# Query projections: block product 6 by seven smaller products, the first query weights scaled on GpSimd

## The chip, the cores and the metric

The kernel runs on one core of one Trainium2 chip. The metric is the device time of one execution in microseconds. The profiler's records of one execution are the profile; its times count from the span's start. The engines are TensorE (PE for its matmuls, PEld for its weight loads), VectorE (DVE), ScalarE (ACT), GpSimd (POOL) and SyncE (SP), which issues most of the DMAs.

## The reference

A cross-attention block and a feed-forward block on 8 batches of 128 tokens, width 512, all in float32 (cut to what matters here):

```python
x = x + xattn(layernorm(x), ctx, mask, ...)     # 32 heads of 128
x = x + ffn(layernorm(x), Wg, Wu, Wd, ag, au, ad)

def xattn(hidden, kv, mask, position_bias, ln_weight, w_q, w_k, w_v, w_out):
    x = rmsnorm(hidden) * ln_weight
    h_q = (x @ w_q.T).reshape(b, lq, 32, 128)   # 512 -> 4096
    h_k = (kv @ w_k.T).reshape(b, lk, 32, 128)
    h_v = (kv @ w_v.T).reshape(b, lk, 32, 128)
    score = softmax(where(mask, h_q . h_k + position_bias, -inf))
    return hidden + (score . h_v).reshape(b, lq, 4096) @ w_out.T
```

The change lies in `h_q`: the projection of the 1024 normalized tokens by `w_q`, whose rows are scaled by `ln_weight`.

## The kernel before

**Block products.** A product of a weight matrix (512 features by 512 columns of one group of four heads) with the tokens (512 features by 1024 tokens) is cut into 2 by 2 blocks and formed from seven block products rather than eight, numbered 1 to 7, with sums of the weights' blocks (`sums_a`, L299: s1, s2, s4 and a21 in place) and of the tokens' blocks (`sums_b` and `token_sums`: t1, t2, t4 and b12 in place). Each block product contracts 256 features, so it is two tiles of 128 head columns, each two matmuls of 128x128 weights by 512 tokens. Products add up in PSUM: product 6 is added to product 1 and so on, and copies or adds take the partial sums out to the head tiles.

A block product may be cut once more in the same way: `inner` (L383) forms it from seven smaller products of 128 by 256 tokens, in seven steps, in the order 2, 1, 5, 6, 3, 7, 4. The steps write two banks in turn (`two` for 2, 5 and 3, `one` for 1, 6, 7 and 4), and after each step VectorE adds the bank to the head. Steps 6, 7 and 4 accumulate on what step 1 left in `one`; steps 5 and 3 in `two` likewise, step 5 starting it anew. So no step can write its bank before VectorE has read the previous step of that bank.

**The stages around the change.** In `first_kv` TensorE forms keys and values of group 0 from the context. Beside it the first norm runs: for each pair of batches VectorE takes moments and small factors of 128x2, ScalarE scales the tokens (`hn`), VectorE transposes each batch in blocks of 32x32, and SP writes the result to DRAM (`turned`) and reads it back turned (`hT`), one batch after another in one queue. When batches i and i+4 are there, VectorE forms the token sums (`h_sums`). All this is in an order written out by hand: `InOrder` keeps each engine's instructions in program order, and tables such as `moments_at` and `sums_at` say behind which tile of `first_kv` each piece comes. ScalarE scales the query weights of group 0 (`weigh_q`, tiles 17 to 20); GpSimd forms their block sums (`combine_rows`) at tile 21.

**The query stage** runs over the eight groups. For group 0 `whole` forms products 1, 6 and 7 in full; for later groups it forms 1 and 6 in full, and `inner_T7` forms product 7 by seven smaller ones. Products 2 to 5 are always formed by smaller ones: `inner_T` forms all four at once, step by step (`quads`, seven steps of four matmuls and three adds each), and its steps run during the next group: one behind each of the four tiles of `whole`, one behind the second, fourth and sixth step of product 7. GpSimd forms the weight sums for the next group meanwhile: four of 128x512 in `combine_rows`, four of 128x128 for product 7 and eight of 128x256 for products 2 to 5 (`pair_rows`); before that ScalarE scales that group's weights in four parts. The sums lie in tiles of the tags of the attention stage, two sets in turn by the group's parity (`q_rows`). The token sums for product 7 (four instructions on VectorE) are formed in group 1, behind the first tile. Finished heads of the group before are stored to DRAM (`store_queries`); three of the four value tiles of group 0 are kept in DRAM meanwhile and come back at the stage's end.

Around the stage, SP's queue carries the weights of the next group, the stores of heads, the first loads of queries and the bias tiles of the attention stage, in program order as buffers come free.

```python
steps = [(i, *blocks[i]) for i in (2, 1, 5, 6, 3, 7, 4)]
for i, r, c in steps:
    for m, (ns, place) in zip(two if i in (2, 5, 3) else one, places):
        for h, n in enumerate(ns):
            multiply(n, i, m[:, h], i in (2, 1, 5) and h == 0)
```

## Time and profile before

| | us |
|---|---|
| median of 3 runs | 1066.57 (1066.43 to 1066.77) |
| the profiled execution | 1067.09 |
| its span, first to last instruction | 1065.2 |
| PE busy | 1055.4 |
| DVE busy | 742.1 |
| ACT busy | 315.5 |
| POOL busy | 521.4 |
| query stage (first query matmul to first key matmul of group 1) | 57.02 to 233.75 |

The granted TensorE clock was full over the whole span. A timeline row gives the start, the time to the last end, the engine, the line, the operation, the tiles written and read, the shape and how many instructions were merged; brackets give the engine's idle time before the row and what ended it. Line L60 is that of the helper that keeps the order, so many instructions carry it; they are told apart by their tiles (`i_q`: banks of products 2 to 5, `sc_q` and `av_q`: the two banks of product 7, `mm_q`: banks of whole products). One float32 matmul is recorded as two passes, so two rows of 128x256 are one matmul.

### The profile page before, as it was taken

What the parts mean: (1) busy time and instruction counts of PE and PEld (TensorE: products, weight loads), DVE (VectorE), ACT (ScalarE), POOL (GpSimd) and SP (SyncE); (2) the same over time, 40 slices, a digit from 0 to 9 for tenths busy, and PEclk for the clock granted to TensorE, in tenths of its full rate; (3) what the DMA queues carried; (4) which work ended last, traced back from release to release, by engine and by line L of the source; (5) the groups of instructions that cost most, each with busy time, mean ns of one, the idle gap of its engine ahead of it and who ended that gap; (6) DMA issues with size and microseconds to landing.
All of it is one profiled execution on the core that took longest, in us unless ns stands there. A gap on an engine that the chain in (4) does not pass through costs nothing.

```text
span 1065.2 us, 14597 instructions
## 1 busy us (share of the span) xinstructions
PE 1055.4 (99%) x5114; PEld 837.6 (79%) x5114; DVE 742.1 (70%) x1362; ACT 315.5 (30%) x874; POOL 521.4 (49%) x551
## 2 busy tenths in 40 slices
PE   9999999999999999999999999999999999999998
PEld 5657777775889798888889769998888865666887
DVE  4686666697778787787787766884544337889852
ACT  2632122205544434444444433221000012333100
POOL 6446664616855565555652275670000336997010
PEclk9999999999999999999999999999999999999999
DMA  9533444386555554564656557774541632110011
GB/s 291 184 134 119 158 161 156 119 289 231 172 199 188 169 179 168 187 199 161 206 171 196 175 202 235 242 254 136 181 138 60 191 108 60 41 54 5 1 40 40
DMA packets 125560, 165.00 MB, mean 155 GB/s; under 512 B 15696, under 2 KB 77392, under 8 KB 125488
## 3 DMA queue, kind: packets, MB, share of 16 engines
q1 hardware_dynamic: 111072, 132.87, 37.8%
q10 hardware_dynamic: 12544, 24.38, 6.5%
q0 software_dynamic: 1872, 6.82, 2.1%
q8 instruction: 41, 0.67, 0.3%
q14 instruction: 31, 0.25, 0.1%
HBM read 106.38 MB, written 57.67 MB: 154 GB/s over the span
## 4 chain that ended last, share of the span: by engine, by line
PE 90%; DVE 4%; DMA 4%; ACT 1%; issue 1%; ACTq 0%; SPq 0%; POOL 0%; DVEq 0%; POOLq 0%
PE i_q L60 9%; PE m L904 9%; PE m L60 7%; PE mm_v L504 7%; PE mm_k L483 7%; PE i_v L432 7%; PE d L1459 6%; PE i L1324 6%; PE i_k L402 6%; PE mm_q L60 5%; PE mm_f L1364 5%; PE av L583 4%; PE sc L537 4%; PE mm_k L60 2%; PE sc_q L60 1%; PE sc L60 1%
## 5 line engine op out<-in xcount | busy, mean ns | idle before, releaser
L60 DVE TENSOR_TENSOR q<-q,i_q 128x512 f32<-128x512 f32 x168 | 94.8, 596 | 52.6 <-PE i_q L60 50.6
L522 POOL TENSOR_TENSOR s<-pb,mneg 128x512 f32<-128x512 f32 x40 | 61.6, 1539 | 90.8 <-DVE p L561 72.1
L550 ACT ACTIVATE s<-s,nmx 128x128 f32<-128x128 f32 x240 | 93.3, 390 | 32.8 <-DVE nmx L545 23.7
L397 DVE TENSOR_TENSOR v<-v,i_v 128x512 f32<-128x512 f32 (+1 forms) x126 | 73.6, 588 | 32.2 <-PE i_v L432 20.0
L588 ACT COPY aT<-av 128x512 f32<-128x512 f32 x60 | 35.1, 585 | 164.3 <-PE av L583 129.7
L397 DVE TENSOR_TENSOR k<-k,i_k 128x512 f32<-128x512 f32 (+1 forms) x105 | 59.8, 587 | 24.7 <-PE i_k L402 24.3
L60 POOL TENSOR_TENSOR s<-pb,mneg 128x512 f32<-128x512 f32 x24 | 36.8, 1534 | 69.5 <-DVE p L561 28.0
L537 PEld LDWEIGHTS sc<-k,q 128*128 128x128 f32 x416 | 53.8, 192 | 6.7 <-issue 4.1
L376 ACT COPY q<-mm_q 128x512 f32<-128x512 f32 x36 | 20.9, 586 | 124.1 <-PE mm_q L60 124.1
L537 PE MATMUL sc<-k,q 128*128 128x128 f32 x416 | 55.3, 275 | 0.0
L504 PE MATMUL mm_v<-wv,ctx_sb 128*128 128x256 f32 x224 | 52.5, 379 | 0.0
L483 PE MATMUL mm_k<-ctx_sb,wk 128*128 128x512 f32 x112 | 52.4, 593 | 0.0
L301 DVE TENSOR_TENSOR S_a<-a 128x256 f32<-128x256 f32 x22 | 9.3, 424 | 57.7 <-DMA a<-att 32.5
L60 PE MATMUL m<-wo,a 128*128 128x256 f32 x200 | 48.5, 380 | 0.8 <-DMA a<-att 0.8
L583 PE MATMUL av<-pT,v 128*128 128x128 f32 x368 | 48.6, 275 | 0.0
L904 PE MATMUL m<-wo,a 128*128 128x256 f32 x200 | 48.4, 379 | 0.0
L1099 POOL TENSOR_TENSOR x<-x,u 128x256 f32<-128x256 f32 x4 | 3.0, 752 | 90.8 <-DVE x L1098 90.8
L60 POOL TENSOR_TENSOR S_q<-wq 128x512 f32<-128x512 f32 x8 | 10.2, 1270 | 75.0 <-ACT wq L60 75.0
L504 PEld LDWEIGHTS mm_v<-wv,ctx_sb 128*128 128x128 f32 x224 | 41.5, 190 | 5.1
L550 ACT ACTIVATION_READ_ACCUMULATOR s<-s,nmx 128x1 f32 x240 | 44.8, 187 | 0.0
L583 PEld LDWEIGHTS av<-pT,v 128*128 128x128 f32 x368 | 44.8, 192 | 0.0
L561 DVE TENSOR_TENSOR p<-s,ri 128x512 f32<-128x512 f32 x52 | 43.5, 836 | 0.9
(408 smaller groups left out, 2735.1 us busy)
## 6 DMA issues: line engine op xcount, KB each, us to landing
queries<-q SPq DMA_DIRECT2D x32, 512.0 KB, 3.5
turned<-tt SPq DMA_DIRECT2D x64, 256.0 KB, 2.4
pT<-turned SPq DMA_DIRECT2D x64, 256.0 KB, 2.9
att<-aT ACTq DMA_DIRECT2D x64, 256.0 KB, 3.0
q<-queries SPq DMA_DIRECT2D x30, 512.0 KB, 4.9
a<-att SPq DMA_DIRECT2D x23, 512.0 KB, 4.1
wq<-in_wqT_dram SPq DMA_DIRECT2D x8, 1024.0 KB, 6.9
wk<-in_wkT_dram SPq DMA_DIRECT2D x7, 1024.0 KB, 5.6
```

Source lines behind the costliest of these rows:

```text
L60: return self.tc.keep_in_program_order(getattr(self.engine, op)(*args, **kw))
L397: vector.tensor_tensor(to, *(base or [to]), out, ADD)
L402: kv_tensor.matmul(out, a[n][i], b[n][i], start=first, stop=True, skip_group_check=True)
L432: kv_tensor.matmul(out[:, bass.ts(k, S)], b[n][i][:, bass.ts(k, S)], a[n][i], start=first and k == 0, stop=True, skip_group_check=True,)
L483: kv_tensor.matmul(out, w[i][:, c, bass.ts(t, P)], src[i][:, c, :], start=(first and c == 0), stop=(c == HC - 1), skip_group_check=True,)
L504: kv_tensor.matmul(out[:, bass.ts(k, HW)], src[i][:, c, bass.ts(2 * t + k, S)], w[i][:, c, :], start=(first and k == 0 and c == 0), stop=( ...
L537: tensor.matmul(sc[:, j, :], qT[:, j, bass.ts(b % 2, S)], kT[j][:, cols], start=True, stop=True)
L550: scalar.activation(s[:, j, :], s[:, j, :], AF.Exp, bias=nmx[:, j : j + 1], accum_out=sm[:, j : j + 1],)
L583: tensor.matmul(av[:, j, :], v[b // 2][:, b % 2, bass.ts(j, P)], pT[:, :, j, :], start=True, stop=True,)
L904: tensor.matmul(m[n], sa[n][:, c, :], wo_t[g][n][:, c, :], start=(g == order[0] and c == 0 and PRODUCTS.index(n) % 2 == 0), stop=(g == ord ...
L1324: nc.tensor.matmul(out, a[n][k], fine_t[n][k], start=first, stop=True, skip_group_check=True)
L1459: nc.tensor.matmul(out, lhs, rhs, start=bank not in started, stop=(i == NP - 1 or n == 8), skip_group_check=True,)
```

## The change

Three things change.

- Product 6 is formed by seven smaller products in all groups but the first (`inner_T6`, in the banks of the whole products), so `whole` forms product 1 alone there. The steps of products 6 and 7 and of the previous group's `quads` (0) are interleaved by a list. The token sums for products 6 and 7 (eight instructions) are formed where those for 7 were.
- GpSimd scales the weights of group 0 itself, at tile 16 of `first_kv`, and forms their block sums and the finer sums right behind it.
- The sums lie in other tiles: other tags for both sets, one more token-sum tile; all four value tiles are kept in DRAM rather than three. The scaling of the next group's weights is placed at other points of the group.

```diff
+    def inner_T6(name, a, b, heads):
+        def place(r, c, m, first):
+            left, to = (heads[r - 1][:, bass.ds(at + (c - 1) * HW, HW)] for at in (0, 512))
+            return [(to, left if first else to, m[:, 0])]
+
+        banks = [[ps_mm.tile([P, 2, HW], F32, tag="mm", name=f"m6{k}_{name}")] for k in range(2)]
+        return inner(name, multiply_T(a, b), (((6,), place),), banks, True)
...
+    q_rows = [row_space((("aT", 2), ("aT", 2), ("pb", 2)), (("s4", 1), ("p", 1)))]
+
+    def q_inner_rows(g, w):
+
+        pieces, single = q_rows[g % 2]
+        a = {}
+        for n in (6, 7) if g else ():
+            quarters = [w[n][:, c, bass.ts(r, P)] for r in range(2) for c in range(2)]
+            a[n] = sums_a(gpsimd, *quarters, *(single[n][:, k] for k in range(3)))
+        a.update(pair_rows(w, pieces))
+        return a
...
-        if 17 <= n < 17 + DC:
-            weigh_q(q_w[0], n - 17)
-        if n == 21:
+        if n == 16:
+            for c in range(DC):
+                gpsimd.tensor_tensor(
+                    q_w[0][:, c], q_w[0][:, c],
+                    lnw_sb[:, c : c + 1].to_broadcast([P, GW]), ALU.mult,
+                )
             rows_q = combine_rows("q0", q_w.pop(0))
+            a_q0 = q_inner_rows(0, rows_q)
...
-            for i in range(1, B // 2):
-                nc.sync.dma_start(kept[i - 1], v[i])
+            for i in range(B // 2):
+                nc.sync.dma_start(kept[i], v[i])
+            q_rows.append(row_space(3 * (("pT", 4),), 2 * (("tt", 2),)))
...
-        tiles = whole(name, *blocks_T(name, w, h_t, heads), 2 if g else 3)
-        a = q_inner_rows(g, w)
+        tiles = whole(name, *blocks_T(name, w, h_t, heads), 1 if g else 3)
+        a = q_inner_rows(g, w) if g else a_q0
...
             if g == 1 and k == 0:
-                h_inner.update(inner_tokens(vector, h_t, 8, q_place, (7,)))
-            if g + 1 < NG and k >= 2:
-                weigh_q(q_w[g + 1], k - 2)
-        for k, _ in enumerate(inner_T7(name, a, h_inner, heads)) if g else ():
-            if k in (1, 3, 5):
-                next(quads)
...
+                h_inner.update(inner_tokens(vector, h_t, 8, q_place, (6, 7)))
+            if g == 0 and k >= 2:
+                weigh_q(q_w[1], k - 2)
+        if g:
+            streams = {
+                6: inner_T6(name, a, h_inner, heads), 7: inner_T7(name, a, h_inner, heads), 0: quads
+            }
+            for k, n in enumerate((6, 6, 0, 6, 6, 0, 7, 6, 0, 7, 6, 0, 6, 7, 7, 0, 7, 7, 7)):
+                next(streams[n])
+                if g + 1 < NG and k in (2, 5, 8, 11):
+                    weigh_q(q_w[g + 1], k // 3)
+                if g + 1 < NG and k == 11:
+                    rows_now = combine_rows(f"q{g + 1}", q_w.pop(g + 1))
+                if k == 15:
+                    store_queries(g - 1, heads_before)
```

More of the change, by code (lines that the diff above doesn't have):

```diff
@@ L701, in weigh_q, with spare, row_space @@
         InOrder(tc, nc.scalar).mul(w[:, c], w[:, c], lnw_sb[:, c : c + 1])
+    def spare(tag, bufs, shape=(2, 2, P)):
+        return work.tile([P, *shape], F32, tag=tag, name=f"rows_{tag}", bufs=bufs)
+    def row_space(tags, single):
+        tiles = [spare(*t) for t in tags]
+        sevens, sixes = (spare(*t, (3, P)) for t in single)
+        return [t[:, k] for t in tiles for k in range(2)], {7: sevens, 6: sixes}
+    q_rows = [row_space((("aT", 2), ("aT", 2), ("pb", 2)), (("s4", 1), ("p", 1)))]
[7 more added lines that the diff above has]
+        return a
     moments_at, roots_at = {7: 0, 8: 1, 10: 2, 12: 3}, {8: 0, 9: 1, 11: 2, 13: 3}
@@ L760, in xattn_ffn_kernel @@
     v = kvs[0][1]
-    kept = [dram.tile([P, 2, GW], F32, name=f"v0_kept_{i}") for i in range(1, B // 2)]
-    def spare(tag, bufs, shape=(2, 2, P)):
-        return work.tile([P, *shape], F32, tag=tag, name=f"rows_{tag}", bufs=bufs)
+    kept = [dram.tile([P, 2, GW], F32, name=f"v0_kept_{i}") for i in range(B // 2)]
     def q_place(n):
-        if n == 7:
-            pieces = [t[:, k] for t in q_seven for k in range(2)]
-        else:
-            pieces = [t[:, k] for t in q_sums for k in range(4)][3 * (n - 2) :]
-        t1, t2, t4 = pieces[:3]
-        return t1, t2, h_t[n][:, 0, slice(8, None)], t4
-    def q_inner_rows(g, w):
-        pieces, single = q_rows[g % 2]
-        a = {}
-        if g:
-            quarters = [w[7][:, c, bass.ts(r, P)] for r in range(2) for c in range(2)]
-            a[7] = sums_a(gpsimd, *quarters, *(single[:, k] for k in range(3)))
-        a.update(pair_rows(w, pieces))
-        return a
+        t1, t2, t4 = q_sums[3 * (n - 2) :][:3]
+        return t1, t2, h_t[n][:, 0, slice(8, None)], t4
     quads, rows_now, h_inner = iter(()), rows_q, {}
@@ L790, in xattn_ffn_kernel @@
         if g == 0:
-            for i in range(1, B // 2):
-                nc.sync.dma_start(kept[i - 1], v[i])
+            for i in range(B // 2):
+                nc.sync.dma_start(kept[i], v[i])
+            q_rows.append(row_space(3 * (("pT", 4),), 2 * (("tt", 2),)))
             q_sums = [
-                acts.tile([P, 4, 8, BS], F32, tag="a", name=f"t_q{k}") for k in range(3)
-            ]
-            even, odd = [spare("s", 3) for _ in range(3)], [spare("tt", 2) for _ in range(2)]
-            odd.append(spare("aT", 2))
-            q_rows = [
-                ([t[:, k] for t in tiles for k in range(2)], single)
-                for tiles, single in (
-                    (even, spare("s4", 1, (3, P))), (odd, spare("aT", 2, (4, P))),
-                )
-            ]
-            q_seven = [
-                work.tile([P, 2, 8, BS], F32, tag="pT", name=f"t_q7{k}", bufs=4) for k in range(2)
-            ]
+                acts.tile([P, 4, 8, BS], F32, tag="a", name=f"t_q{k}") for k in range(4)
+            ] + [work.tile([P, 2, 8, BS], F32, tag="pT", name="t_q", bufs=4)]
+            q_sums = [t[:, k] for t in q_sums for k in range(t.shape[1])]
         w, heads, name = rows_now, [], f"q{g}"
-        tiles = whole(name, *blocks_T(name, w, h_t, heads), 2 if g else 3)
-        a = q_inner_rows(g, w)
+        tiles = whole(name, *blocks_T(name, w, h_t, heads), 1 if g else 3)
+        a = q_inner_rows(g, w) if g else a_q0
         for k, _ in enumerate(tiles):
@@ L818, in xattn_ffn_kernel @@
             if g == 1 and k == 0:
-                h_inner.update(inner_tokens(vector, h_t, 8, q_place, (7,)))
-            if g + 1 < NG and k >= 2:
-                weigh_q(q_w[g + 1], k - 2)
-        for k, _ in enumerate(inner_T7(name, a, h_inner, heads)) if g else ():
-            if k in (1, 3, 5):
-                next(quads)
-            if g + 1 < NG and k in (0, 2):
-                weigh_q(q_w[g + 1], 2 + k // 2)
-            if k == 2 and g + 1 < NG:
-                rows_now = combine_rows(f"q{g + 1}", q_w.pop(g + 1))
-            if k == 5:
-                store_queries(g - 1, heads_before)
+                h_inner.update(inner_tokens(vector, h_t, 8, q_place, (6, 7)))
[13 more added lines that the diff above has]
+                    store_queries(g - 1, heads_before)
         if g == 0:
@@ L839, in xattn_ffn_kernel @@
     store_queries(NG - 1, heads)
-    for i in range(1, B // 2):
+    for i in range(B // 2):
         v[i] = acts.tile([P, 2, GW], F32, tag="a", name=f"v0_back_{i}")
-        nc.sync.dma_start(v[i], kept[i - 1])
+        nc.sync.dma_start(v[i], kept[i])
     gpsimd, vector, kv_tensor = nc.gpsimd, nc.vector, nc.tensor
```

## The prediction

> **What bounds the kernel now.** I read the page first, then the busy time by stretch, then the rows of TensorE, VectorE and GpSimd by time where the change works.

> ```profile
> PE 1055.4 (99%) x5114; PEld 837.6 (79%) x5114; DVE 742.1 (70%) x1362; ACT 315.5 (30%) x874; POOL 521.4 (49%) x551
> PE 90%; DVE 4%; DMA 4%; ACT 1%; issue 1%; ACTq 0%; SPq 0%; POOL 0%; DVEq 0%; POOLq 0%
> ```

> TensorE works nearly without a break. The edited query stage lies from 57.02 to 233.75 us; by stretch (sum, then busy PE, PEld, DVE, ACT, POOL):

> ```profile
> 67.33:89.30 21.97, 21.97 (x88) 16.34 (x86) 16.72 (x30) 6.66 (x12) 19.54 (x25) 1.00 0.12 49
> 111.27:133.25 21.98, 21.98 (x88) 16.34 (x87) 14.27 (x29) 4.81 (x8) 12.26 (x17) 1.00 0.40 144
> ```

> A group takes 21.97 us and PE is busy for all of it: no slack on PE, 5 to 8 on DVE. So a matmul less is time gained, and a wait of PE is time lost; nothing later takes it back.

> ```profile
> 131.95 0.59 PE L60 MATMUL i_q<-t_q,wq 128*128 128x256 f32 x2
> 132.38 0.59 PE L60 MATMUL i_q<-t_q,S_q 128*128 128x256 f32 x2
> 132.82 0.59 PE L60 MATMUL sc_q<-t_q,wq 128*128 128x256 f32 x2
> ```

> Each row is one 128x256 matmul (two passes), 0.43 us from start to start; a 128x512 one takes 0.86.

> **Part 1, fewer matmuls.** Product 6 of a group was 4 matmuls of 128x512, 3.44 us; now it is 7 of 128x256, 3.02 us. Seven groups: 7 x 0.43 = 3.0 us gained. Two ACT copies per group go (0.59 each), seven DVE adds come (0.41 each, as on product 7's banks): DVE goes from 14.3 to 17.2 us of some 22, no bound by itself. Four more GpSimd sums of 128x128 (0.46 each) make its 12.3 us about 14.1; the scaling ahead of them is no longer behind product 6's copies, so they start earlier. All hidden under 22 us of PE.

> **Part 2, the new order of steps.** The seven steps go (2, 1, 5, 6, 3, 7, 4). The last two accumulate in one bank: DVE must have read it after step 7 before PE may run step 4. Before, product 7 ran 7 7 Q 7 7 Q 7 7 Q 7 (Q: a step of the previous group's block sums, 1.72 us on PE), so a Q stood between. Now the list ends 7 7 Q 7 7 7: steps 3, 7, 4 back to back.

> ```profile
> 133.02 1.02 DVE L60 TENSOR_TENSOR q<-q,i_q 128x512 f32<-128x512 f32 x2 [0.17 <-PE i_q L60]
> 133.95 0.41 DVE L60 TENSOR_TENSOR q<-q,sc_q 128x256 f32<-128x256 f32 x1
> ```

> Let T be the time when Q's last matmul has its turn behind it (132.82 above). DVE gets Q's second half at T+0.20 and is through at T+1.13 (133.02, 133.95). The add of step 3 follows, then that of step 7, 0.33 apart as on the two product-7 banks at 131.36 and 131.69: step 7's starts at T+1.46 and ends at T+1.87. PE starts 0.05 behind a DVE read (read ended 231.60, matmul 231.65), at T+1.92; it was ready at T+0.86. It waits 1.06 us in each of seven groups, 7.4 us, and behind it on PE stands the next group's product 1. Bounds: were DVE idle, step 7's result would come at T+1.06 and the wait be 0.66 (4.6 in all); with dependent adds 0.52 apart (126.18 to 126.70, same banks) 1.43 (10.0). I take 1.06, since those two banks' adds go to different heads. Parts 1 and 2 together: +4.4 (+1.6 to +7.0).

> That PE does stop for this, in the tail where no product 7 lies between:

> ```profile
> 231.08 0.59 PE L60 MATMUL i_q<-hT,S_q 128*128 128x256 f32 x2
> 231.65 0.70 PE L60 MATMUL i_q<-t_q,wq 128*128 128x256 f32 x2
> ```

> 0.57 in place of 0.43, even with 0.86 us of the other half's matmuls as cover.

> **Part 3, GpSimd scales the first query weights.** ACT loses 4 x 0.66 us that nobody waited for. GpSimd was idle from 28.78 to 43.75; the weights landed at 24.25. Now four scalings (taken as the 128x512 row, 1.26), four sums of the same size and eight of 128x256 (0.73) fill 28.8 to about 44.6. That moves GpSimd's work off the h sums at 47.45 to 55.9, and onto norm 1's small VectorE instructions:

> ```profile
> 26.45 1.11 DVE L60 SCALAR_TENSOR_TENSOR nm<-mv,rr 128x2 f32<-128x2 f32 x1
> ...
> 29.21 0.17 DVE L60 TENSOR_SCALAR rr<-mv 128x2 f32<-128x2 f32 x1
> 29.29 0.16 DVE L60 RECIPROCAL rr<-rr 128x2 f32<-128x2 f32 x1
> 29.48 0.16 DVE L60 SCALAR_TENSOR_TENSOR nm<-mv,rr 128x2 f32<-128x2 f32 x1
> ```

> The same instruction takes 0.16 us with GpSimd idle and 1.11 with GpSimd busy: it ended at 27.56, just behind a GpSimd row that ended at 27.54. Four such lie ahead of the first transpose (29.21, 29.48, 31.29, 31.56). With GpSimd rows ending every 1.24 us they end at about 30.0, 31.2, 33.65 and 35.0, and the first transpose starts at 34.9, not 31.64: +3.3 us. Behind it SP's queue writes and reads the transposed blocks through DRAM with no slack: blocks 3, 4 and 5 landed at 45.3, 47.4 and 49.9, 2.3 apart, so block 5 lands at 49.9 + 3.3 = 53.2. DVE forms three h sums on it (0.57 each) before it may add v (0.68) and free PE's bank: 55.6.

> ```profile
> 47.45 5.30 DVE L60 TENSOR_TENSOR hT<-hT 128x256 f32<-128x256 f32 x6 [3.19 <-DMA hT<-turned]
> 53.49 3.69 PE L60 MATMUL mm_v<-S_v,ctx_sb 128*128 128x256 f32 x16 [1.32 <-DVE v L60]
> ```

> PE was ready at 52.17 and waited 1.32 us, since these six sums took 5.30 us with GpSimd beside them where the next six took 3.42. It would now wait 3.5: +2.2. Bounds: without the delay, 49.9 + 1.7 + 0.7 = 52.3, a wait of 0.15, -1.2; with a whole 1.27 for each of the four, 5.1 of delay, +4.0. Taken: +2.2.

> **Part 4, token sums for product 6.** In the first step of group 1 DVE now forms eight sums, not four, while GpSimd works:

> ```profile
> 71.97 1.44 DVE L60 TENSOR_TENSOR t_q<-hT 128x256 f32<-128x256 f32 x1
> 73.45 1.38 DVE L60 TENSOR_TENSOR t_q<-hT,t_q 128x256 f32<-128x256 f32 x1
> 74.75 0.67 DVE L60 TENSOR_TENSOR hT<-hT 128x256 f32<-128x256 f32 x1
> ```

> From the group's start (67.33 above): they begin at +4.64; two at 1.4 beside long GpSimd rows, six at 0.6 beside short ones: done at +11.0. Then Q's adds (1.54) and product 6's step 2 (0.41): +13.0. PE reaches product 6's step 5, which overwrites that bank, at 2 x 1.72 + 2 x 1.72 + 2 x 0.43 + 1.72 = +9.46. Wait 3.5 us, behind which everything on PE stands; before, PE had product 6 whole as cover and did not stop. Bounds: eight at 0.42 (no GpSimd): 0.5; all at 1.44: 8.7. I take 3.5, GpSimd's sums of 128x128 being short.

> [...]

> **Moved and added DMAs.** One more 512 KB store of v and one more load: the first pair of loads landed by 235.0, first use at 257.93; 20 us of cover. One bias load now waits for a sum tile and stands on SP ahead of group 6's stores, but its tile is free before those stores' data is. Cost 0; if the cover were gone, one load's pace, 1.3 us.

> **Sum.** 4.4 + 2.2 + 3.5 = +10.1 on the profiled execution: span 1065.2 to 1075.3. That execution took 1067.09 us, 0.5 above the median of 1066.57. Forecast for the median: 1076.7.

> **Rivals.**
> - *The count decides* (8%): PE finds the bank read, because DVE runs further ahead than I think. It decides once the wait per group is under 0.43 us. Then -3.0, and with the h sums free of GpSimd -1.2: 1062.4, faster. For it: DVE has slack over a group. Against it: the wait is one DVE latency at least, 0.66.
> - *GpSimd's early work disturbs nothing* (12%): the small instructions slip in between; -1.2 in place of +2.2 and 0.5 in place of 3.5: 4.4 - 1.2 + 0.5 = +3.7, 1070.3. For it: 0.17 us instructions need little. Against: three rows of 0.93 to 1.11.
> - *DVE falls behind in every group* (10%): from product 6's step 2 on, PE has 5 x 1.72 + 14 x 0.43 = 14.6 us of work and DVE 5 x 1.54 + 14 x 0.41 = 13.4 or more; a further 0.5 us per group gives +3.5, 1080.2.
> - *Forecast* (70%): 1076.7, by itself 1073 to 1079.

> Less than 0.2% (2.1 us) can't be told from no change here. Range 1070.0 to 1079.8: forecast and second rival, and half of the third. Faster 0.08, same 0.02, slower 0.90.

> **What would show it.** After: PE idle some 1.0 us before the last matmul on sc_q in each of groups 1 to 7; a group of 22.6 us; one wait of 3 us or more on product 6's bank in group 1; the wait on v at 3.5 us in place of 1.32, with the small instructions at 1 us. I am wrong if groups take 21.5 us, or if the first transpose starts at 31.6 as before.

## The result

The changed kernel is slower: 1076.63 us median (1074.88 to 1077.20, 4 runs) against 1066.57 (1066.43 to 1066.77), a ratio of 1.0091, 95% interval 1.0074 to 1.0109. The profiled execution took 1076.73 us, its span 1075.0 against 1065.2. The forecast of 1076.7 was met, but three of its terms were mis-sized, one of them because a loss was not in it at all; the errors nearly cancelled. The page of the changed kernel, busy time by engine and the chain that ended last:

```profile
PE 1055.8 (98%) x5156; PEld 846.0 (79%) x5156; DVE 757.6 (70%) x1415; ACT 305.1 (28%) x856; POOL 535.1 (50%) x583
PE 88%; DVE 7%; DMA 3%; issue 1%; ACT 1%; ACTq 0%; SPq 0%; POOL 0%; DVEq 0%; POOLq 0%
```

VectorE's share of the chain goes from 4% to 7%: TensorE now waits for it. TensorE has less to do, yet its busy time rises by 0.4 us, the first sign that some matmuls became slower. By stretch, group 1 and a later group (length, then busy PE, PEld, DVE, ACT, POOL, then granted clock, DMA share and GB/s):

```profile
66.77:95.00 28.23, 23.87 (x93) 18.43 (x92) 22.28 (x42) 5.51 (x10) 25.54 (x35) 0.94 0.12 49
95.00:117.74 22.74, 21.83 (x93) 17.41 (x92) 16.67 (x35) 3.73 (x6) 17.07 (x26) 1.00 0.38 140
```

A group is 0.77 us longer than its 21.97 before, although PE works 0.14 less in it; group 1 is longer by another 5.49, at a lower clock. That is 7 x 0.77 + 5.49 = 10.9 us in the query stage. It began 0.5 us earlier (56.49 against 57.02) and the later stages take another 0.5 less: +9.8, the difference of the spans.

The end of a group, TensorE by time (start, us, tiles, shape; brackets: idle time and what ended it), and then VectorE:

```profile
115.27 0.59 PE L60 MATMUL av_q<-hT,rows_s 128*128 128x256 f32 x2
115.70 0.59 PE L60 MATMUL sc_q<-hT,wq 128*128 128x256 f32 x2
117.20 0.70 PE L60 MATMUL sc_q<-t_q,wq 128*128 128x256 f32 x2 [0.91 <-DVE q L60]
117.74 1.45 PE L60 MATMUL mm_q<-hT,wq 128*128 128x512 f32 x3
```

```profile
115.47 1.02 DVE L60 TENSOR_TENSOR q<-q,i_q 128x512 f32<-128x512 f32 x2 [0.18 <-PE i_q L60]
116.41 0.41 DVE L60 TENSOR_TENSOR q<-q,av_q 128x256 f32<-128x256 f32 x1
116.74 0.41 DVE L60 TENSOR_TENSOR q<-q,sc_q 128x256 f32<-128x256 f32 x1
117.94 0.42 DVE L60 TENSOR_TENSOR q<-q,sc_q 128x256 f32<-128x256 f32 x1 [0.79 <-PE sc_q L60]
```

Step 7 on `sc_q` starts at 115.70. Step 4 goes into the same bank and could follow at 116.13; it starts at 117.20, 0.05 after VectorE's read of step 7 (116.74 + 0.41), which stood behind the adds of the block sums. The wait is 1.07 us from start to start. The next matmul starts 0.54 instead of 0.43 later, a slower restart of 0.11, so a stop costs 1.18 in all.

Group 1, the same two engines:

```profile
74.54 1.89 PE L60 MATMUL i_q<-t_q,rows_aT 128*128 128x256 f32 x8
79.88 1.20 PE L60 MATMUL m_q<-t_q,rows_tt 128*128 128x256 f32 x4 [3.45 <-DVE q L60]
80.91 0.91 PE L60 MATMUL i_q<-t_q,rows_aT 128*128 128x256 f32 x2
81.61 1.06 PE L60 MATMUL i_q<-t_q,rows_pb 128*128 128x256 f32 x2
...
85.19 0.59 PE L60 MATMUL i_q<-hT,rows_aT 128*128 128x256 f32 x2
```

```profile
71.44 1.44 DVE L60 TENSOR_TENSOR t_q<-hT 128x256 f32<-128x256 f32 x1
72.91 1.39 DVE L60 TENSOR_TENSOR t_q<-hT,t_q 128x256 f32<-128x256 f32 x1
74.22 0.68 DVE L60 TENSOR_TENSOR hT<-hT 128x256 f32<-128x256 f32 x1
...
79.33 0.93 DVE L60 TENSOR_TENSOR q<-q,m_q 128x256 f32<-128x256 f32 x2
```

VectorE reads `m_q` (product 6's bank) only at 79.33, behind eight token sums, two of them at 1.4 us; TensorE stands idle for 3.45 us. But after it the same two passes that take 0.59 at 85.19 take 1.06 at 81.61. The stretches of the same execution show why (columns as above, the third last is the granted clock):

```profile
79.50:81.00 1.50, 1.12 (x5) 0.87 (x6) 1.40 (x4) 0.00 (x0) 1.50 (x3) 1.00 0.00 0
81.00:84.60 3.60, 3.60 (x11) 2.87 (x10) 2.32 (x6) 0.00 (x0) 3.52 (x6) 0.53 0.00 0
84.60:95.00 10.40, 9.49 (x44) 8.04 (x43) 8.94 (x20) 0.00 (x0) 10.09 (x15) 1.00 0.32 129
```

For 3.6 us TensorE had 0.53 of its clock: 3.6 x 0.47 = 1.7 us lost, while TensorE waited for nothing. The wait itself cost 3.6 us from start to start (the matmul at 79.88 could have followed at 76.26) and its slower restart 0.17 (1.03 us to the next row, where four such passes take 0.86); together this is the 5.5 us of group 1.

Last, norm 1's small instructions and the end of the first stage, VectorE and then TensorE:

```profile
29.15 0.60 DVE L60 TENSOR_SCALAR rr<-mv 128x2 f32<-128x2 f32 x1
...
29.85 0.89 DVE L60 SCALAR_TENSOR_TENSOR nm<-mv,rr 128x2 f32<-128x2 f32 x1
...
32.38 0.35 DVE L60 TENSOR_SCALAR rr<-mv 128x2 f32<-128x2 f32 x1
...
32.84 1.25 DVE L60 SCALAR_TENSOR_TENSOR nm<-mv,rr 128x2 f32<-128x2 f32 x1
34.01 1.29 DVE L60 STREAM_TRANSPOSE tt_h<-hn 128x512 f32<-128x512 f32 x2
...
50.99 1.22 DVE L60 TENSOR_TENSOR hT<-hT 128x256 f32<-128x256 f32 x3 [1.09 <-DMA hT<-turned]
52.13 1.28 DVE L60 TENSOR_TENSOR v<-v,mm_v 128x512 f32<-128x512 f32 x2
```

```profile
52.96 3.69 PE L60 MATMUL mm_v<-S_v,ctx_sb 128*128 128x256 f32 x16 [0.84 <-DVE v L60]
```

The four small instructions do wait (0.60, 0.89, 0.35 and 1.25 in place of 0.17 and 0.16; each ends 0.02 to 0.03 us behind a GpSimd row, which end at 29.72, 30.72, 32.71 and 34.07), and the first transpose is 2.4 us later. Yet the wait on v fell from 1.32 to 0.84.

### The profile page after: what moved, and what is told of

It is laid out like the page before. It is cut to its first block, busy times and chain, and to the rows that moved or that the text cites. A ratio compares the mean times of both kernels' runs of the same rounds, so it can differ in the third digit from the quotient of the medians.

```text
span 1075.0 us, 14757 instructions
## 1 busy us (share of the span) xinstructions
PE 1055.8 (98%) x5156; PEld 846.0 (79%) x5156; DVE 757.6 (70%) x1415; ACT 305.1 (28%) x856; POOL 535.1 (50%) x583
## 4 chain that ended last, share of the span: by engine, by line
PE 88%; DVE 7%; DMA 3%; issue 1%; ACT 1%; ACTq 0%; SPq 0%; POOL 0%; DVEq 0%; POOLq 0%
PE m L913 9%; PE i_q L60 9%; PE m L60 7%; PE mm_v L512 7%; PE mm_k L491 7%; PE i_v L440 7%; PE d L1468 6%; PE i L1333 6%; PE i_k L402 6%; PE mm_f L1373 5%; PE av L591 4%; PE sc L545 4%; PE mm_q L60 3%; PE m_q L60 2%; DVE q L60 1%; PE mm_k L60 1%
## 5 line engine op out<-in xcount | busy, mean ns | idle before, releaser
L60 DVE TENSOR_TENSOR q<-q,i_q 128x512 f32<-128x512 f32 x168 | 94.9, 596 | 39.1 <-PE i_q L60 36.0
L60 POOL TENSOR_TENSOR s<-pb,mneg 128x512 f32<-128x512 f32 x24 | 36.7, 1534 | 71.6 <-DVE p L60 42.0
L376 ACT COPY q<-mm_q 128x512 f32<-128x512 f32 x22 | 12.7, 586 | 133.6 <-PE mm_q L60 133.5
L60 PE MATMUL m<-wo,a 128*128 128x256 f32 x200 | 48.5, 380 | 0.7 <-DMA a<-att 0.7
L60 POOL TENSOR_TENSOR S_q<-wq 128x512 f32<-128x512 f32 x8 | 10.2, 1273 | 64.2 <-ACT wq L60 58.9
```

What stands on the lines that cost most here:

```text
L60: return self.tc.keep_in_program_order(getattr(self.engine, op)(*args, **kw))
```

## The experiments

Product 6 stays in seven smaller ones in all of them, and GpSimd scales the first query weights where nothing else is said. They ran on three chips. On the first, where the kernel before took 1067.44 us (23 runs), ran the order alone, the place alone, both, and part 3 undone as well; on the second (1067.01, 23 runs) ran both once more, four sums, six sums and values first; on the third (1067.26, 10 runs) ran part 3 undone with that wait gone, and one more profile each of six sums and of part 3 undone as well. Ratios are to the kernel before on the same chip. Where a time of groups 0 and 1 is given, it is TensorE's from its first query matmul to the end of group 1 in the profile, which leaves out what varies before and behind.

**Order of the steps alone.** A step of the block sums stands between steps 7 and 4 of product 7 again, and `store_queries` moves behind it:

```diff
-(6, 6, 0, 6, 6, 0, 7, 6, 0, 7, 6, 0, 6, 7, 7, 0, 7, 7, 7)
+(6, 6, 0, 6, 6, 0, 7, 6, 7, 6, 0, 6, 7, 7, 0, 7, 7, 0, 7)
-                if k == 15:
+                if k == 17:
```

> The changed kernel with one entry of the list of steps moved: a step of the block sums (0) from ninth place to the place before the last step of product 7, so that steps 7 and 4 are apart again; the store of the heads goes behind it. Theory (the wait between steps 7 and 4 costs 1.07 us and about 0.1 of restart in each of groups 1 to 7): seven times 1.2, 8.4 us less, median about 1068.3, a group of 21.5 us, no idle time of TensorE before the last sc_q matmul. Rival (VectorE as a whole is behind; the wait only moves to another bank): less than 4 us gained, above 1072.5, with a wait elsewhere in each group. Waits on product 6's bank in group 1 (3.5 us) and on v (0.84) stay.

Measured: 1070.38 us, ratio 1.0027 (1.0017 to 1.0037), span 1067.4. A group by stretch, then group 1's wait:

```profile
116.02:137.59 21.57, 21.57 (x94) 17.48 (x93) 16.59 (x36) 3.73 (x6) 14.23 (x21) 1.00 0.41 147
```

```profile
80.52 1.51 PE L60 MATMUL m_q<-t_q,rows_tt 128*128 128x256 f32 x4 [3.46 <-DVE q L60]
81.82 1.06 PE L60 MATMUL i_q<-t_q,rows_aT 128*128 128x256 f32 x2
```

PE is busy for the whole group: 22.74 - 21.56 = 1.18, times seven 8.3 us. The stage started 0.63 later, which leaves 7.6, the difference of the spans (1075.0 to 1067.4). So the order costs 1.18 per group; against the kernel before the groups are 0.41 shorter, which is part 1's gain. Group 1 keeps its wait and its half clock. In the medians the gain is 6.3 us and not the 8.4 expected: on this chip the kernel before also took 0.9 more, and the stage began 0.63 later. The rival's mark, above 1072.5, was not reached.

**Place of the token sums alone.** Product 6's four sums go into group 0, where GpSimd is done, and product 7's four behind that group's tiles:

```diff
-            if g == 1 and k == 0:
-                h_inner.update(inner_tokens(vector, h_t, 8, q_place, (6, 7)))
+            if g == 0 and k == 4:
+                h_inner.update(inner_tokens(vector, h_t, 8, q_place, (6,)))
...
+            h_inner.update(inner_tokens(vector, h_t, 8, q_place, (7,)))
```

> The changed kernel with the eight token sums of products 6 and 7 formed in group 0 (product 6's behind the fifth tile, product 7's behind the last one), where GpSimd is idle. Theory (these sums beside GpSimd hold up VectorE and with it product 6's bank in group 1; the slow TensorE rows behind that wait come from the wait): the 3.45 us wait goes, and with it the stretch of half clock (about 1.7 us): 5 to 5.8 us less, median about 1071.2, sums at 0.42 us each. Rival (the half clock is not due to the wait): only 3.6 less, 1073.0, and slow rows remain near 81 to 84 us. The waits between steps 7 and 4 stay.

Measured: 1071.91 us, ratio 1.0043 (1.0028 to 1.0058), span 1070.1, mean clock 1.000. TensorE in group 1, where it stopped before:

```profile
75.12 1.89 PE L60 MATMUL i_q<-t_q,rows_aT 128*128 128x256 f32 x8
76.85 1.03 PE L60 MATMUL m_q<-t_q,rows_tt 128*128 128x256 f32 x4
77.71 0.59 PE L60 MATMUL i_q<-t_q,rows_aT 128*128 128x256 f32 x2
```

The wait is gone and the half clock with it; the sums take 0.42 us each in their new place. The spans differ by 4.9 us, which is 5.5 less the 0.6 by which this stage began later. The groups stay at 22.74. The median lies 0.7 above the expected 1071.2; the rival (1073.0, with slow rows left) is out. Each edit took away its own loss and left the other.

**Both.** Both edits together:

> Both edits together: the moved step and the earlier token sums. If the two waits are separate and all that was lost: 1076.6 - 8.4 - 5.4 = about 1062.8, faster than the kernel before by 3.0 us for the seven fewer matmul slots and 0.5 to 0.8 for the shorter wait on v. Rival (something else in the change costs time, hidden so far): above 1065.

Measured: 1064.96 us, ratio 0.9974 (0.9965 to 0.9984), and on a second chip:

> The same program as the kernel with both undone (order of the steps and place of product 6's token sums), run once more so that the next three stand beside it on one chip. Expected: its time within 0.15% of its earlier 1064.96 us where the kernel before is also where it was; groups 1 to 7 at 21.56 us each, no wait above 0.3 us inside the query stage, granted clock 1.00 throughout the stage, and the wait on v of the last pair at 1.5 to 1.8 us.

1064.08 us, ratio 0.9967 (0.9956 to 0.9977). Groups 1 to 7 take 21.56 us each with no stop. So without these two losses the change is a gain of some 0.3%, and its order and its place for the sums turned it into a loss. The expected 1062.8 was missed by 2.2 and 1.3 us, and the first median lies at the rival's bound of 1065. Of the 2.2, 0.9 is the slower chip (by the kernel before) and 0.8 the wait on v, which is 1.66 and 1.77 us in these two profiles and not the 0.84 of the changed kernel's; the rest was not traced.

**Undoing part 3 as well.** ScalarE scales the first weights, and the row sums are formed at tile 21, as in the kernel before:

```diff
-        if n == 16:
-            for c in range(DC):
-                gpsimd.tensor_tensor(q_w[0][:, c], q_w[0][:, c], ..., ALU.mult)
+        if 17 <= n < 17 + DC:
+            weigh_q(q_w[0], n - 17)
+        if n == 21:
             rows_q = combine_rows("q0", q_w.pop(0))
```

> As the run with both edits, and ScalarE scales the first query weights again, with GpSimd's sums for group 0 at their old place (tile 21). Theory from the profile after: GpSimd is beside the h sums again, the wait on v is 1.3 us and not 0.8, the query stage starts 0.5 us later: 0.5 us more than the run with both edits. Rival, as the prediction had it: norm 1's small instructions are free again, so 2.2 us less.

Measured: 1065.62 us, ratio 0.9977 (0.9968 to 0.9987), wait on v 2.01. The rival's 2.2 us less did not come. The median is 0.7 above the kernel with both undone, near the 0.5 expected, but the intervals overlap: here it is not settled what part 3 is worth. The ten executions fall in two sorts: mean clock 0.999 or 1.000 in six (1064.9 us on average) and 0.998 in four (1066.4).

**How long a wait brings the half clock?** From the kernel with both undone, four or six token sums go back to group 1 (the changed kernel has eight there). Four:

```diff
+            if g == 1 and k == 0:
+                h_inner.update(inner_tokens(vector, h_t, 8, q_place, (7,)))
...
-            h_inner.update(inner_tokens(vector, h_t, 8, q_place, (7,)))
```

> Against the kernel with both undone: the four token sums of product 7 go back to the start of group 1, product 6's four stay in group 0. Model of VectorE in that stretch (reads 0.25, adds 1.4 while GpSimd works): TensorE waits about 1.15 us on product 6's first bank in group 1. Theory (the granted clock halves only after a wait of some 3.5 us): no rows at half clock follow, the whole costs 1.1 to 1.3 us over the kernel with both undone. Rival (any wait in this place is followed by the half clock, because the work behind it is what starts slowly): passes 0.43 apart for some 3.5 us behind the wait, and 2.8 to 3.1 us in all.

Measured: 1066.04 us, ratio 0.9986 (0.9976 to 0.9995), 2.0 above the kernel with both undone in the medians, between the theory's price and the rival's. The profiles settle it: groups 0 and 1 take 33.27 us against 31.87, +1.40, which is the theory's 1.1 to 1.3 and the restart. TensorE:

```profile
77.53 1.20 PE L60 MATMUL m_q<-t_q,rows_tt 128*128 128x256 f32 x4 [1.07 <-DVE q L60]
78.56 0.59 PE L60 MATMUL i_q<-t_q,rows_aT 128*128 128x256 f32 x2
```

A wait of 1.07 us (1.25 from start to start), 0.17 for the restart, and full clock behind it (1.00 from 77.5 to 95.0). The 0.25 us that the model gives a read was the author's estimate; VectorE's adds of 128x256 from a bank took 0.41 in the changed kernel. Six (product 6's four and two of product 7's):

```diff
-            if g == 0 and k == 4:
+            if g == 1 and k == 0:
                 h_inner.update(inner_tokens(vector, h_t, 8, q_place, (6,)))
+                third_and_fourth()
...
-            h_inner.update(inner_tokens(vector, h_t, 8, q_place, (7,)))
+            vector.tensor_tensor(t1, b12, b11, SUB)
+            vector.tensor_tensor(t2, b22, t1, SUB)
```

> Against the kernel with both undone: six token sums at the start of group 1 (product 6's four and two of product 7's). By the same model TensorE waits about 2.35 us on product 6's first bank. Theory (half clock only after a wait of some 3.5 us): passes stay 0.215 apart behind the wait, +2.3 to 2.6 us over the kernel with both undone. Rival (half clock after any wait of more than about 2 us): a stretch at half clock of some 3.5 us follows, and +4.1 to 4.4 us. With the changed kernel's eight sums (wait 3.45, half clock) and the four sums (wait about 1.15) this brackets where the half clock begins.

Measured: 1068.61 us, ratio 1.0007 (0.9997 to 1.0018), +4.5 over the kernel with both undone (+4.27 in groups 0 and 1). By stretch from the end of the wait:

```profile
79.45:80.30 0.85, 0.85 (x3) 0.62 (x4) 0.85 (x2) 0.00 (x0) 0.77 (x2) 0.84 0.00 0
80.30:83.70 3.40, 3.40 (x10) 2.65 (x10) 2.40 (x6) 0.00 (x0) 3.32 (x6) 0.54 0.01 2
```

My theory, that it takes some 3.5 us, falls: a wait of 2.26 was followed by the half clock too, and the rival's price (4.1 to 4.4) is the one that came. One more execution of the same kernel:

> The kernel with six token sums in group 1, profiled once more. Its first profile had a wait of 2.26 us and a stretch at clock 0.54 from 80.3 to 83.7 us; of its ten executions eight had a mean clock of 0.999 or less, two of 1.000. Theory (the clock is judged over windows of some 3.4 us that run free of the kernel): the wait is again 2.2 to 2.4 us; the half clock begins at another distance from it, 0 to 4 us after its end, lasts about 3.4 us again, and in about two executions of ten is not there at all. Rival (the clock falls at a fixed idle time): half clock begins within 0.2 us of the same distance, 0.9 us after the wait's end.

1068.24 us, with a wait of 2.27 us that ended at 79.60, and again by stretch:

```profile
79.60:80.85 1.25, 1.25 (x5) 0.95 (x6) 1.25 (x3) 0.00 (x0) 1.17 (x3) 1.00 0.00 0
80.85:84.25 3.40, 3.40 (x10) 2.69 (x9) 2.21 (x6) 0.00 (x0) 3.32 (x5) 0.50 0.01 2
```

It lasts 3.4 us again, but begins some 1.25 us after the wait, where in the first profile the clock had fallen within 0.85 (0.84 of full speed there). The delay is not fixed to the wait. What the profiles record of the clock's changes stands in the last section. Then the kernel with part 3 undone as well:

> The kernel with both undone and ScalarE scaling the first weights, profiled once more. Its ten executions had a mean clock of 1.000 or 0.999 six times (1064.2 to 1065.8 us) and 0.998 four times (1066.0 to 1066.7). Theory (a wait of about 2.1 us, the one on v, sometimes tips the clock to one half for some 3.4 us, by where it falls in a free-running time): if this execution's clock is 0.998, passes 0.43 apart stand for about 3.4 us soon after the wait on v and nowhere else behind the first 5 us; if it is 1.000, there are none, and the wait is of the same 2.0 to 2.2 us. Rival (the 0.998 comes from another place in the run): with 0.998, rows 0.43 apart stand elsewhere, far from the wait on v.

1064.74 us, mean clock 1.000, a wait on v of 2.17 us from start to start and no slow passes after it. So this execution decides nothing; where the 0.998 of the other four comes from was not recorded.

**Values first.** From the kernel with both undone, the token sums of the second pair of h go behind the last pair's v in VectorE's queue:

```diff
-    sums_at = {21: (0,), 22: (1,), 25: (2, 3)}
+    sums_at = {21: (0,), 25: (1, 2, 3)}
```

> The kernel with both undone, and VectorE's two token sums of the second pair of h moved behind the last pair's v (from two tiles after it is fetched to the place of the third and fourth pair's). Theory (the wait on v that is left, 1.5 to 1.8 us there, is VectorE's: h sums stand ahead of the v adds in its queue): the wait on v goes to below 0.5 us, the query stage starts 1.0 to 1.8 us earlier, and the time falls by as much: about 0.9985 of the kernel with both undone. Rival (the wait is the transfer chain's: block 5 lands late, whatever VectorE does): wait on v unchanged within 0.3 us, time the same within 0.3 us. A third way: the sums of the second pair of h come late for the first products of group 0, which then wait; the time is the same or up to 2 us more.

Measured: 1062.47 us, ratio 0.9949 (0.9935 to 0.9964), the fastest version. That is 0.9985 of the kernel with both undone, as expected. TensorE at the end of the first stage in the kernel with both undone (second chip), then in this one, each with VectorE below it:

```profile
48.74 3.62 PE L60 MATMUL mm_v<-S_v,ctx_sb 128*128 128x256 f32 x16
54.13 3.69 PE L60 MATMUL mm_v<-S_v,ctx_sb 128*128 128x256 f32 x16 [1.77 <-DVE v L60]
57.65 2.74 PE L60 MATMUL mm_q<-hT,wq 128*128 128x512 f32 x6
```

```profile
52.16 1.22 DVE L60 TENSOR_TENSOR hT<-hT 128x256 f32<-128x256 f32 x3 [1.10 <-DMA hT<-turned]
53.30 1.28 DVE L60 TENSOR_TENSOR v<-v,mm_v 128x512 f32<-128x512 f32 x2
```

```profile
48.57 7.07 PE L60 MATMUL mm_v<-S_v,ctx_sb 128*128 128x256 f32 x32
55.48 3.60 PE L60 MATMUL mm_q<-hT,wq 128*128 128x512 f32 x8
```

```profile
50.57 0.69 DVE L60 TENSOR_TENSOR v<-v,mm_v 128x512 f32<-128x512 f32 x1
52.30 0.69 DVE L60 TENSOR_TENSOR v<-v,mm_v 128x512 f32<-128x512 f32 x1 [1.04 <-PE mm_v L60]
```

The two rows of 16 have become one of 32 without a stop; the stage starts 2.2 us earlier, and the span is 2.0 shorter. The wait was VectorE's order: it stood at the sums of block 5, which waits for a transfer until 52.16, and its v adds came behind them, at 53.30; now the first comes at 50.57.

**Part 3 undone with that wait gone.**

```diff
-        if n == 16:
-            for c in range(DC):
-                gpsimd.tensor_tensor(q_w[0][:, c], q_w[0][:, c], ..., ALU.mult)
+        if 17 <= n < 17 + DC:
+            weigh_q(q_w[0], n - 17)
+        if n == 21:
```

> The kernel with the second pair's token sums behind the last pair's v, with part 3 undone in it: ScalarE scales the first query weights one chunk a tile and the row sums are formed at tile 21, as in the kernel before. In the kernel with both undone that edit cost 0.66 us in the medians, and its wait on v was 2.17 instead of 1.82 us. Theory (part 3 reaches the time through the wait on v alone, and that wait is gone here): same within 0.4 us of the kernel it is made from (1062.47), no wait above 0.5 us on v, query stage starting within 0.3 us of 55.48. Rival (the scalings delay something else, the chain of block 5 or the row sums that group 0 needs): 0.5 to 1.0 us slower, with the query stage or a product of group 0 starting later by that.

Measured: 1063.98 us, ratio 0.9969 (0.9957 to 0.9980), so 1.5 us above the last one in the medians and 1.2 in the span. The two ran on different chips (the kernel before is 0.25 apart) and the intervals of their ratios just overlap, but all seven executions lie above all four of the other. The theory falls; the rival comes true, larger than its 0.5 to 1.0. VectorE's nine sums of h, first with GpSimd scaling (idle by then), then with ScalarE scaling:

```profile
52.90 3.47 DVE L60 TENSOR_TENSOR hT<-hT 128x256 f32<-128x256 f32 x9
```

```profile
53.07 4.94 DVE L60 TENSOR_TENSOR hT<-hT 128x256 f32<-128x256 f32 x9
```

0.39 us a sum against 0.55, which leaves VectorE 1.6 us behind. In group 0 TensorE then idles 0.23 us at 61.19: ScalarE's copy of a bank stands behind a small instruction that waits for VectorE. In group 1 it stops on product 6's bank: the last three token sums of product 7 now fall beside GpSimd's sums for group 1 and take 1.4 to 1.5 us each instead of 0.42. TensorE in the second kernel:

```profile
76.60 1.19 PE L60 MATMUL m_q<-t_q,rows_tt 128*128 128x256 f32 x4 [0.52 <-DVE q L60]
```

Groups 0 and 1 are 1.35 us longer. So moving GpSimd's work out of the h sums is a gain of part 3 here, which the changed kernel hides.

## Why the prediction came true, and where it did not

- **Part 1, -3.0: right.** Without its stops a group takes 21.56 instead of 21.97 us, 0.41 x 7 = 2.9. VectorE's 16.7 us and GpSimd's 14 were hidden as argued.
- **Part 2, +7.4: mechanism and wait right, the cost of stopping mis-sized.** The wait of 1.06 was 1.07 from start to start, in each of the seven groups, by the path named (block sums' adds, step 3, step 7, 0.05 to TensorE). Left out was the slower restart, 0.11 for the matmul behind the stop. The cost is 1.18 x 7 = 8.3, as the order alone showed. Parts 1 and 2 together gave +5.4, not +4.4, inside their bounds.
- **Part 3, +2.2: mis-sized, by 2.7 us in this execution.** The step "the first transpose starts at 34.9, +3.3" gave +2.4: GpSimd's scalings took 1.0 each (four in 4.03), not the 1.26 of the sums, and the four small instructions lost 0.61 us each on average, about half a GpSimd row. The step "blocks 2.3 apart, so block 5 lands 3.3 later" failed: it landed 1.1 later (50.97 against 49.90), the chain through DRAM having made up the rest, so it had some slack. And the h sums on it took 0.42 us each, not 0.57, since GpSimd was idle by then; the prediction named that effect but charged the old price. The wait on v came out between 0.8 and 1.8 us in the idle times of the profiles with this part and the old order of the sums (1.32 before), and the stage began between 0.5 us earlier and 0.6 later than before, nowhere near +2.2. (With part 3 undone and the same old order, the two profiles have 2.01 and 2.00, so the wait also varies by what part 3 doesn't touch.) With the wait on v away, part 3 is a gain of 1.2 to 1.5, by one pair of kernels.
- **Part 4, +3.5: the wait right, the loss 2 us larger.** TensorE waited 3.45 us, on the bank named, for sums of the sizes named (two at 1.4, six at some 0.65). The half clock behind it, 1.7 us, was not foreseen: the prediction took a wait to cost its own length. Putting the sums elsewhere took all 5.5 away.
- **Moved DMAs, 0: nothing showed.** From 225 to 320 us, where the kept values and the bias tiles are used, TensorE waits for no transfer in the changed kernel (0.2 us for one before). One profile of the kernel with both undone does show 1.32 us on a transfer of attention weights at 284.35, the other 0.16 there: that one varies by execution.

So -0.5 + 5.4 + 5.5 and -0.5 later, against 2.2 + 4.4 + 3.5: the sums agree within 0.3 us, because part 3 was set 2.7 too high and parts 2 and 4 were 1.0 and 2.0 too low. That the total was met so closely is luck: it would have confirmed a working that was wrong in three terms.

With GpSimd busy the small instructions took up to 1.25 us in the changed kernel, and the same sums of h 0.55 in place of 0.39 in the last pair of kernels. The upper bound of part 3, a whole row of 1.27 lost by each of the four, was not reached in the changed kernel: the largest loss was 1.09 us and the mean 0.61, about half of a GpSimd row of 1.0 to 1.28.

## What to carry to other kernels

Count what an extra stop of TensorE costs by more than its length: here 0.11 to 0.17 us for a restart, and 1.7 more where the half clock followed (behind waits of 3.45 us, and of 2.3 us in 8 of 11 executions, by their mean clock). Between two steps that accumulate in one bank put work for as long as VectorE's adds take to get there: here a step of the block sums, 1.72 us, took away a wait of 1.07. And on a queue in program order, put what another engine waits for ahead of what waits for a transfer: that one line was worth 1.6 us in the medians here (2.0 in the spans), and it took the whole to 0.9949 of the kernel before.

## What the runs showed of the hardware

TensorE's granted clock fell to one half for some 3.4 us after waits of 3.45 (two kernels) and 2.3 us (one kernel, two profiles), beginning 0.6 to 1.3 us after the end of the wait; passes of 128x256 then start 0.43 us apart instead of 0.215. After 1.07 us (four sums), and after 1.8 and 2.0 us on v (both undone; part 3 undone as well), the profiles show none.

```profile
76.61:80.02 3.41, 1.15 (x6) 0.55 (x4) 3.31 (x8) 0.00 (x0) 3.25 (x7) 1.00 0.00 0
80.02:83.43 3.41, 3.41 (x9) 2.71 (x9) 2.56 (x6) 0.00 (x0) 3.33 (x6) 0.50 0.01 2
...
50.84:54.25 3.41, 1.46 (x7) 0.95 (x5) 3.38 (x6) 0.00 (x0) 3.33 (x5) 1.00 0.65 166
54.25:57.66 3.41, 3.36 (x16) 3.00 (x17) 3.34 (x8) 0.00 (x0) 1.45 (x2) 1.00 0.99 333
```

TensorE idled for 0.66 of the first window and 0.57 of the third. With the run's end left out, the windows ahead of the half clock were idle for 0.63 to 0.78 in the four profiles that have it, and no window for more than 0.57 in the nine others (table). That the clock is judged over such windows, as an expectation above has it, fits these shares; no record shows it by itself. An estimate from them: if some 2 us of idle time in one window (0.57 to 0.63 of 3.413 us) bring the half clock, a wait of 3.45 us does so at some 80% of the places where a window can begin, one of 2.26 at about half, and one below 1.9 at none. The mean clock listed for every execution can be held against that:

| kernel | TensorE's longest wait from 20 us to group 1's end in its profile, us | largest idle share of one window, the run's end left out | executions with mean clock 0.998 or less |
|---|---|---|---|
| order alone | 3.46 | 0.78 | 8 of 9 |
| changed kernel | 3.45 | 0.65 | 3 of 4 (the other 0.999, and the fastest) |
| six sums (two profiles) | 2.26 and 2.27 | 0.66 and 0.63 | 8 of 11 |
| part 3 undone as well (two profiles) | 2.01 and 2.00 | 0.57 and 0.53 | 4 of 11 |
| both undone (two chips) | 1.66 and 1.77 | 0.41 and 0.42 | 1 of 17 |
| place alone | 1.41 | 0.41 | 0 of 4 |
| kernel before (three chips) | 1.32 | 0.39 | 9 of 56 |
| four sums | 1.07 | 0.50 | 0 of 10 |
| part 3 undone, values first | 0.52 | 0.35 | 0 of 7 |
| values first | 0.33 | 0.37 | 0 of 4 |

0.002 of a run is 2 us, the size of the loss. A mean of 0.999 needs no such stretch: where values come first and part 3 is undone, the profile's clock falls only 1.5 us before the run's end. The upper rows fit the estimate roughly. The 9 of 56 and the 1 of 17 do not follow from waits of 1.32 to 1.77 us; where the clock fell in executions that were not profiled isn't shown.
